# Grouped attention with normalization on one core: the inverses' transfers, the first batch's normalization, the last batch's sums and the general path rewritten

## The chip, the cores and the metric

The kernel runs on one core of a Trainium2 chip. The metric is the device time of one execution in microseconds (us). Before the change it is 1826.72 us, the median of 4 runs (1825.81 to 1828.08).

The engines are named as in the profile: PE is TensorE (its weight loads are listed apart, as PEld), DVE is VectorE, ACT is ScalarE, POOL is GpSimd, and SP is SyncE, which here issues transfers. A q behind a name (SPq) marks what the engine's sequencer does itself: it issues a transfer, waits for a semaphore, branches.

## What is computed

The input x has 32 batches of 256 channels and 32 x 32 positions. Each batch is normalized in 32 groups of 8 channels, projected to queries, keys and values of 8 heads of 32 channels, and goes through causal attention that also hides the position itself. The result is added to x. All of it is in float32.

```python
x = x + _L0_conv_ref(_gn(x), q_w, q_b, kv_w, kv_b)

def _gn(v, G=32, eps=1e-5):
    g = v.reshape(B_, G, C_ // G, H_, W_)
    m = jnp.mean(g, axis=(2, 3, 4), keepdims=True)
    s = jnp.var(g, axis=(2, 3, 4), keepdims=True)
    return ((g - m) / jnp.sqrt(s + eps)).reshape(v.shape)

def _L0_conv_ref(x, q_w, q_b, kv_w, kv_b):      # N_HEADS = 8, MASK_CENTER = True
    q = jnp.einsum('oc,bcs->bos', q_w, xf) + q_b[None, :, None]
    kv = jnp.einsum('oc,bcs->bos', kv_w, xf) + kv_b[None, :, None]
    ...
    mask = jnp.tril(jnp.ones((S, S), dtype=x.dtype), -int(MASK_CENTER))
    scores = jnp.einsum('bhqd,bhkd->bhqk', q, k) / jnp.sqrt(jnp.asarray(dk, x.dtype))
    scores = jnp.where(mask == 0, jnp.asarray(-10000.0, x.dtype), scores)
    attn = jax.nn.softmax(scores, axis=-1)
    attn = jnp.where(mask == 0, jnp.asarray(0.0, x.dtype), attn)
    out = jnp.einsum('bhqk,bhkd->bhqd', attn, v)
```

## The kernel before

**Two paths.** The function `unshifted` computes every batch with plain exponentials, without a maximum taken off first. It checks on the way that all sums of exponentials lie within 1e-20 and 1e20, and ends with the count `outside` of partitions where one doesn't. Each engine reads that count (line 784). If it is over zero, the general path `shifted` computes everything again, with the maximum taken off (line 785). With the inputs given here the count is zero, so `shifted` is jumped over. Its instructions stand in the program between that branch and the closing barrier.

**The tiling.** Channels lie on the 128 partitions, in two groups g of four heads each. The 1024 positions are two halves hf of 512 queries, and eight blocks k of 128 keys. One quarter n of a batch is a pair (g, hf), so n runs from 0 to 3. Scores are held transposed, with keys on partitions, so that their exponentials e can be multiplied with the values at once.

**Visits.** A batch is worked through in N = 12 visits, six for each group (line 531 on). A visit takes a full piece and a half piece of the scores: f is a list of pieces by half and key block, h holds half pieces. For one group the full and half pieces are (f00, f02), (f01, h10), (f10, h11), (f13, h20), (f14, h21), (f15, f16), where the first digit is the half and the second the key block, or the key block and the part for h. The multiplication with the values follows one visit later, by the list `products`. So visits 6 to 11 belong to the second group.

**The order of work.** The engines' order is written by hand: `when(i, f)` puts a step into visit i, behind that visit's scores (`at`) or behind its value products (`after`). A visit number counts from the batch's first one. PE, DVE, ACT and POOL follow that order strictly. SP takes transfers in the order of the program.

**The normalization of a batch.** DVE takes means and variances by channel (lines 167 and 168). PE averages them over each group of 8 by a product with `avg` (tile pm). ACT writes the mean with its sign changed (line 175), DVE the spread of the channels (dev, lines 183 to 187), PE averages that (tile pv), and POOL raises the variance to the power -0.5 (line 205 or 207), which gives rstd. Batch 0 has forms of its own: DVE takes the variance out of the averaging product (line 197), ACT prepares `less_mean` for one of the four pieces (line 583) and scales it (line 219), and DVE writes the other three pieces of xn (line 221). Between these PE turns the three weight matrices (`turn_weights`, four transposes each, line 136), the first of them ahead of the variance's product. `keep_busy(n)` gives PE n products without use (line 143).

**Sums of exponentials.** For batches 0 to 30 DVE adds the pieces of a quarter as they come (line 377). POOL's transfers fold the 128 partitions' sums of a quarter to 32 rows (`fold`, line 393), SP's stack the four quarters in one tile (`stack`, line 399), and DVE sums the rest (lines 406 and 407). `invert` takes the inverses (line 445) and turns them (line 447). SP writes them to DRAM in four transfers (line 450) and reads them back in sixteen, four for each quarter, each spread over 32 partitions (line 458). The four tiles rb have one buffer each. `finish` multiplies the numerators with rb on DVE (line 490), adds the bias and x (line 491) and has SP write the quarter out (line 494). The steps of batch b reach into the visits of batch b + 1: `invert` at its visit 8, the finishes behind its visits 13 to 15. For batch 30 all of this is some visits earlier.

**The last batch, 31.** There PE sums the pieces listed in `by_pe` itself, by products with a column of ones spread to 32 (`sum_keys`, line 414, tiles pd), and DVE the others. A `None` in the lists of `sums` stands for what DVE has added up. `invert_here` takes the inverses of one quarter on DVE alone, without a transfer (lines 478, 480, 481). Quarter 0 is multiplied on POOL (`quotient_aside`, line 500) and finished on ACT (`out_aside`). `end_last` inverts quarter 3 in two parts, finishes one, checks the inverses (lines 438 and 439), takes the minimum, has PE add up the result over partitions (line 523), finishes the other part, and writes `outside` (line 526).

Of the kernel before, what the change touches and what calls it, by code (L numbers as in the profile page):

```python
# [17 lines left out]
P = 128  # L18
HD = 32
# [12 lines left out]
def tile_norm_attention_residual(  # L32
# [65 lines left out]
    def unshifted():  # L98
# [71 lines left out]
        def norm_mean(b):  # L170
            mv = live["mv", b]
            pm = misc(f"pm_{b}")
            product(pm[:, :NG], avg, mv[:, :, 0])
            mean = small.tile([P, NG], F32, tag="mean", name=f"mean_{b}")
            nc.scalar.activation(mean, pm[:, :NG], AF.Identity, scale=-1.0)
            live["minus_mean", b], live["pm"] = mean, pm

        def norm_deviation(b):
# [3 lines left out]
            if b == 0:  # L182
                nc.vector.tensor_sub(dev, mv[:, :, 0], live["pm"][:, :NG])
            else:
                nc.vector.tensor_add(dev, mv[:, :, 0], minus_mean)
# [4 lines left out]
        def norm_variance(b):  # L190
            pv = misc(f"pv_{b}")
            product(pv[:, :NG], avg, live.pop(("dev", b)))
            rstd = small.tile([P, NG], F32, tag="rstd", name=f"rstd_{b}")
            live["rstd", b] = rstd
            if b == 0:

                nc.vector.tensor_scalar_add(rstd, pv[:, :NG], 1e-5)
                return
            nc.scalar.activation(rstd, pv[:, :NG], AF.Identity, bias=eps)

        def norm_rstd(b):
            rstd = live["rstd", b]
            if b == 0:

                nc.gpsimd.tensor_tensor(rstd, rstd, power, ALU.pow)
                return
# [4 lines left out]
        def norm_apply(b, hf, g):  # L211
# [6 lines left out]
            if (b, hf, g) == (0, 0, 1):  # L218
                nc.scalar.activation(xn, live["less_mean"], AF.Identity, scale=rstd)
            elif b == 0:  # L220
# [220 lines left out]
        def invert(b):  # L441
# [6 lines left out]
            spread = dram.tile([4, 4, HALF], F32, tag="inv", name=f"inverses_{b}")  # L448
            for n in range(4):
                nc.sync.dma_start(  # L450
                    out=spread[n].rearrange("(a j) (m c) -> (j m) a c", a=2, c=HD),
                    in_=turned[n * HD : (n + 1) * HD].rearrange("p (a c) -> p a c", a=2),
                )
            for n in range(4):

                rb = inverses(b, n)
                for j in range(4):
                    nc.sync.dma_start(  # L458
                        out=rb[j * HD : (j + 1) * HD], in_=spread[n, j : j + 1].broadcast_to([HD, HALF]),
                    )  # L460

        def inverses(b, n):
            if (b, n) == (B - 2, 3):
                live["rb_last"] = work.tile([P, 4, HALF], F32, tag="folded", bufs=1, name="rb_last")
            if (b, n) < (B - 2, 3) or (b, n) == (B - 1, 0):
                live["rb", b, n] = work.tile([P, HALF], F32, tag="rb", bufs=4, name=f"rb_{b}_{n}")
            else:
                live["rb", b, n] = live["rb_last"][:, n if b == B - 1 else 0, :]
            return live["rb", b, n]

        def invert_here(b, n, within=slice(0, HALF)):


            if within.start == 0:
                inverses(b, n)
# [6 lines left out]
                live["rb", b, n][:, within].rearrange("p (k r) -> p k r", r=HD),  # L482
# [3 lines left out]
        def finish(b, n, within=slice(0, HALF)):  # L486
            g, hf = divmod(n, NH)
            cols = slice(hf * HALF + within.start, hf * HALF + within.stop)
            num, rb, xt = live["num", b, n], live["rb", b, n][:, within], live["x", b]
# [6 lines left out]
        def quotient_aside(b, n):  # L496

            g, hf = divmod(n, NH)
            rb = live["rb", b, n]
# [3 lines left out]
        def out_aside(b, n):  # L503
            g, hf = divmod(n, NH)
            cols = slice(hf * HALF, (hf + 1) * HALF)
            rb = live["rb", b, n]
# [5 lines left out]
        def end_last(b):  # L512
# [4 lines left out]
            finish(b, 3, both[1])  # L517
# [6 lines left out]
            finish(b, 3, both[0])  # L524
# [19 lines left out]
        by_pe = [pc for n, m in ((5, 0), (6, 1), (7, 0), (9, 1), (10, 0), (11, 0)) for pc in products[n][m:]]  # L544
# [24 lines left out]
        with tc.manual_schedule(engines={ENG.PE, ENG.Activation, ENG.DVE, ENG.Pool}):  # L569
# [8 lines left out]
            for g in range(NG):  # L578
                norm_channels(0, g)
            norm_mean(0)  # L580

            live["less_mean"] = work.tile([P, 4, HALF], F32, tag="folded", bufs=1, name="less_mean")[:, 0, :]
            nc.scalar.activation(
                live["less_mean"], live["x", 0][:, 1, :HALF], AF.Identity, bias=live["minus_mean", 0][:, 1:2]
            )
            turn_weights(0)
            norm_deviation(0)
            norm_variance(0)
            norm_rstd(0)
            for hf in range(NH):  # L590
                for g in range(NG):
                    norm_apply(0, hf, g)
                if hf == 0:
                    for n in (1, 2):
                        turn_weights(n)
                    keep_busy(3)
# [9 lines left out]
            for b in range(B):  # L606
# [7 lines left out]
                if not last:  # L614
# [10 lines left out]
                    for n in every:  # L625
                        when(first + ((N + 9, N + 9, N + 10, N + 10) if late else FINISH)[n], lambda b=b, n=n: finish(b, n), after)
                else:
                    when(first + 3, lambda: sums(0, [None], False), after)
                    when(first + 7, lambda: sums(1, [None, *products[5]], False), after)
                    when(first + 9, lambda: sums(2, [None, *products[6][1:], *products[7]], False), after)  # L630
                    when(first + 5, lambda b=b: invert_here(b, 0), after)
# [4 lines left out]
                    when(first + 10, lambda b=b: invert_here(b, 2), after)  # L636
                    when(first + 11, lambda b=b: finish(b, 2), after)
            for i in range(B * N + 1):
# [5 lines left out]
                if i == B * N:  # L644

                    sums(3, pcs, False)
                for pc in pcs:
                    values((i - 1) // N, pc, i <= (B - 1) * N or pc not in by_pe)
                if i == B * N - 1:
                    sums(3, [*pcs, products[9][1], None])  # L650
# [11 lines left out]
    def shifted():  # L662

        with ExitStack() as inner:
            pool = inner.enter_context(tc.tile_pool(name="g_pool", bufs=1))
            rows = inner.enter_context(tc.tile_pool(name="g_rows", bufs=2))
            ps_a = inner.enter_context(tc.tile_pool(name="g_ps_a", bufs=2, space=PSUM))
            ps_b = inner.enter_context(tc.tile_pool(name="g_ps_b", bufs=2, space=PSUM))
# [143 lines left out]
```

## Time and profile before

| what | before |
|---|---|
| median of 4 runs | 1826.72 us (1825.81 to 1828.08) |
| the profiled execution | 1825.96 us, its span 1824.3 us |
| PE busy | 1810.7 us, 99% of the span |
| DVE busy | 1650.4 us, 90% |
| ACT busy | 1479.9 us, 81% |
| POOL busy | 798.4 us, 44% |
| rb read back (line 458) | 492 transfers of 64.0 KB, 2.7 us from issue to landing |
| inverses written (line 450) | 124 transfers of 8.0 KB, 2.7 us |

The span is the time from the first to the last instruction in the trace, and the execution's own time has 1.7 us more around it. A row of the timeline reads: start in us, time taken in us, engine, line of the kernel, operation, the tile written <- the tiles read, shapes, and in brackets the idle time before it with what ended it. The page's groups of instructions give count and mean duration for a line. The chain of waits follows back from the last instruction to what released each step. "Granted clock" is the share of its full clock that the throttle gives PE; here it is 0.998 over the span.

### The profile page before, as it was taken

What the parts mean: (1) busy time and instruction counts of PE and PEld (TensorE: products, weight loads), DVE (VectorE), ACT (ScalarE), POOL (GpSimd) and SP (SyncE); (2) the same over time, 40 slices, a digit from 0 to 9 for tenths busy, and PEclk for the clock granted to TensorE, in tenths of its full rate; (3) what the DMA queues carried; (4) which work ended last, traced back from release to release, by engine and by line L of the source; (5) the groups of instructions that cost most, each with busy time, mean ns of one, the idle gap of its engine ahead of it and who ended that gap; (6) DMA issues with size and microseconds to landing.
All of it is one profiled execution on the core that took longest, in us unless ns stands there. A gap on an engine that the chain in (4) does not pass through costs nothing.

```text
span 1824.3 us, 54461 instructions
## 1 busy us (share of the span) xinstructions
PE 1810.7 (99%) x23210; PEld 926.5 (51%) x23210; DVE 1650.4 (90%) x1759; ACT 1479.9 (81%) x1862; POOL 798.4 (44%) x776
## 2 busy tenths in 40 slices
PE   9999999999999999999999999999999999999997
PEld 5554555555554555545555545555454555555543
DVE  4699999999999999999999999999999999999987
ACT  6888878888778888788887888887888878888785
POOL 1453443535434445344354354443443544534432
PEclk9999999999999999999999999999999999999999
DMA  3457676676776676766767667767666676676662
GB/s 122 74 98 135 134 146 116 130 143 129 143 132 126 135 133 133 155 112 129 141 134 144 120 131 137 132 139 147 120 132 133 135 148 116 131 142 130 121 123 73
DMA packets 85226, 235.08 MB, mean 129 GB/s; under 512 B 27760, under 2 KB 28784, under 8 KB 69104
## 3 DMA queue, kind: packets, MB, share of 16 engines
q0 software_dynamic: 15872, 97.53, 39.8%
q1 hardware_dynamic: 69104, 133.99, 26.0%
q8 instruction: 184, 3.01, 0.7%
q14 instruction: 66, 0.54, 0.1%
HBM read 66.85 MB, written 34.57 MB: 56 GB/s over the span
## 4 chain that ended last, share of the span: by engine, by line
PE 97%; DVE 2%; DMA 0%; SPq 0%; issue 0%; ACT 0%; DVEq 0%
PE sT L283 31%; PE acc L369 27%; PE pp L157 26%; PE ppv L157 13%; DVE e L377 0%; SPq L458 0%; DMA rb<-inverses 0%; DMA x<-in_x_dram 0%; PE pv L157 0%; DVE rb_last L491 0%; DVE rows L407 0%; DVE turned L406 0%; DVE st L167 0%; DVE rb_last L490 0%; DVE turned L478 0%
## 5 line engine op out<-in xcount | busy, mean ns | idle before, releaser
L344 ACT ACTIVATE e<-sT 128x1024 f32<-128x1024 f32 x768 | 744.8, 1022 | 270.6 <-PE sT L283 219.5
L377 DVE TENSOR_TENSOR e<-e,e 128x1536 f32<-128x1536 f32 x377 | 633.2, 1680 | 18.4 <-POOL shift L209 0.5
L377 DVE TENSOR_TENSOR e<-e,eh 128x1024 f32<-128x1024 f32 x379 | 522.7, 1393 | 123.6 <-PE acc L369 102.2
L297 POOL TENSOR_SCALAR_AFFINE_SELECT e<-e 128x512 f32<-128x512 f32 (+1 forms) x257 | 378.3, 1472 | 556.6 <-ACT e L344 553.4
L283 PE MATMUL sT<-q,k 32*128 32x256 f32 (+3 forms) x7168 | 606.8, 458 | 0.0
L283 PEld LDWEIGHTS sT<-q,k 32*128 32x128 f32 x7168 | 444.8, 184 | 152.9 <-ACT eh L342 65.2
L157 PE MATMUL pp<-xn,wT 128*32 128x512 f32 x4096 | 492.2, 598 | 0.0
L369 PE MATMUL acc<-e,v 128*32 128x512 f32 (+2 forms) x4096 | 400.7, 486 | 0.0
L342 ACT ACTIVATE eh<-sT 128x1024 f32<-128x1024 f32 x384 | 396.3, 1032 | 0.0
L393 POOL DMA_DIRECT2D e<-e x248 | 203.0, 826 | 395.0 <-DMA e<-e 278.1
L157 PE MATMUL ppv<-wT,xn 128*32 128x256 f32 x4096 | 247.5, 382 | 0.0
L369 PEld LDWEIGHTS acc<-e,v 128*32 128x32 f32 x4096 | 132.6, 110 | 223.3 <-issue 191.5
L369 PE MATMUL acc<-eh,v 128*32 128x256 f32 x3072 | 224.4, 379 | 0.0
L157 PEld LDWEIGHTS pp<-xn,wT 128*32 128x32 f32 x4096 | 107.2, 109 | 219.4 <-issue 205.7
L369 PEld LDWEIGHTS acc<-eh,v 128*32 128x32 f32 x3072 | 98.5, 110 | 164.2 <-issue 153.2
L157 PEld LDWEIGHTS ppv<-wT,xn 128*32 128x32 f32 x4096 | 120.4, 109 | 102.7 <-issue 32.4
L297 POOL TENSOR_SCALAR_AFFINE_SELECT eh<-eh 128x512 f32<-128x512 f32 x128 | 167.3, 1307 | 0.3
L223 ACT ACTIVATE xn<-x,shift,rstd 128x512 f32<-128x512 f32 x124 | 102.9, 830 | 0.0
L491 DVE SCALAR_TENSOR_TENSOR rb<-rb,v_bias_col,x 128x512 f32<-128x512 f32 x123 | 92.7, 754 | 4.4
L237 ACT ACTIVATE k<-pp,qk_bias 128x512 f32<-128x512 f32 x128 | 89.4, 699 | 2.2 <-PE pm L157 1.1
L237 ACT ACTIVATE q<-pp,qk_bias 128x512 f32<-128x512 f32 x128 | 89.6, 700 | 1.0 <-PE pp L157 1.0
L407 DVE TENSOR_REDUCE rows<-turned 128x16 f32<-128x512 f32 x124 | 85.1, 686 | 4.3
(75 smaller groups left out, 667.0 us busy)
## 6 DMA issues: line engine op xcount, KB each, us to landing
e<-e POOLq DMA_DIRECT2D x124, 512.0 KB, 6.0
x<-in_x_dram SPq DMA_DIRECT2D x64, 512.0 KB, 6.2
e<-e POOLq DMA_DIRECT2D x124, 256.0 KB, 4.6
folded<-e SPq DMA_DIRECT2D x124, 256.0 KB, 3.0
out_dram<-rb SPq DMA_DIRECT2D x124, 256.0 KB, 4.5
rb<-inverses SPq DMA_DIRECT2D x492, 64.0 KB, 2.7
inverses<-inv_turned SPq DMA_DIRECT2D x124, 8.0 KB, 2.7
out_dram<-rb_last SPq DMA_DIRECT2D x3, 256.0 KB, 2.0
```

The costliest lines, as they stand in the source:

```text
L157: nc.tensor.matmul(out[part], lhsT=lhsT[:, part], rhs=rhs, start=start, stop=stop, skip_group_check=True)
L223: nc.scalar.activation(xn, xt, AF.Identity, bias=live["shift", b][:, g : g + 1], scale=rstd)
L237: nc.scalar.activation(live[key][:, cols], pp, AF.Identity, bias=qk_bias[:, n, g : g + 1], scale=(SCALE, 1.0)[n],)
L283: return nc.tensor.matmul(pair[:, cols], lhsT=live["k", b, g][rows, kb * P : (kb + 1) * P], rhs=live["q", b, g][rows, hf * HALF + of.start ...
L297: nc.gpsimd.affine_select(out=diagonal, in_=diagonal, pattern=[[0, heads.stop - heads.start], [0, n], [1, P]], compare_op=ALU.is_gt, fill= ...
L342: exp = nc.scalar.activation(eh.rearrange("p (n bank) q -> p bank n q", n=2), short, AF.Exp)
L344: nc.scalar.activation(e[:, 2 * a : 2 * a + 2, :], pairs[a], AF.Exp)
L369: nc.tensor.matmul(acc[HD * j : HD * (j + 1), of], lhsT=live["v", b][:, kb, h * HD : (h + 1) * HD], rhs=e[:, j, cols], start=first, stop=l ...
L377: nc.vector.tensor_add(total[:, :, of], total[:, :, of], e[:, :, cols])
L393: nc.gpsimd.dma_start(out=total[:rows], in_=total[rows : 2 * rows], accum_op=ALU.add)
L407: nc.vector.tensor_reduce(live["rows", b][:, j * HALF // HD : (j + 1) * HALF // HD], turned.rearrange("p (k r) -> p k r", r=HD), AX.X, ALU ...
L491: nc.vector.scalar_tensor_tensor(rb, rb, v_bias_col[:, g : g + 1], xt[:, g, cols], ALU.add, ALU.add)
```

## The change

- **Start.** The special forms of batch 0 go, except that DVE still writes xn, now all four pieces. The variance comes to ACT, the product `shift` is formed on POOL as in other batches, and all three `turn_weights` stand behind `norm_rstd`, with a `keep_busy(3)` ahead of the variance and one behind the weights.
- **Inverses.** One transfer writes them to DRAM and four read them back, one for each of the four head rows, into one tile rb of all quarters with one buffer. The last batch uses a tile of the tag `folded` for all its quarters.
- **Last batch.** f13 of the second group is summed by PE in place of DVE, and f02 by DVE in place of PE. The sums for quarter 3 are made in another order. Quarter 0 is inverted one visit later, quarter 2 ahead of the value products of its visit in place of behind them. In `end_last` both finishes come ahead of the check.
- **General path.** It is written in loops over value blocks, groups, q and k, query blocks, heads and key blocks, with 14 matrix products in the text, in place of one loop over batches around code that is written out.

```diff
@@ norm_deviation, norm_variance, norm_rstd, norm_apply
-            if b == 0:
-                nc.vector.tensor_sub(dev, mv[:, :, 0], live["pm"][:, :NG])
-            else:
-                nc.vector.tensor_add(dev, mv[:, :, 0], minus_mean)
+            nc.vector.tensor_add(dev, mv[:, :, 0], minus_mean)
...
+            nc.scalar.activation(rstd, pv[:, :NG], AF.Identity, bias=eps)
             live["rstd", b] = rstd
-            if b == 0:
-
-                nc.vector.tensor_scalar_add(rstd, pv[:, :NG], 1e-5)
-                return
-            nc.scalar.activation(rstd, pv[:, :NG], AF.Identity, bias=eps)
...
-            if (b, hf, g) == (0, 0, 1):
-                nc.scalar.activation(xn, live["less_mean"], AF.Identity, scale=rstd)
-            elif b == 0:
+            if b == 0:
                 nc.vector.tensor_scalar(xn, xt, live["minus_mean", b][:, g : g + 1], rstd, ALU.add, ALU.mult)
@@ invert
-            spread = dram.tile([4, 4, HALF], F32, tag="inv", name=f"inverses_{b}")
-            for n in range(4):
+            spread = dram.tile([2, 4, 2, HALF], F32, tag="inv", name=f"inverses_{b}")
+            nc.sync.dma_start(
+                out=spread.rearrange("a n j (m c) -> (n j m) a c", c=HD), in_=turned.rearrange("p (a c) -> p a c", a=2),
+            )
+            live["rb", b] = work.tile([P, 4, HALF], F32, tag="rb", bufs=1, name=f"rb_{b}")
+            for h in range(4):
                 nc.sync.dma_start(
-                    out=spread[n].rearrange("(a j) (m c) -> (j m) a c", a=2, c=HD),
-                    in_=turned[n * HD : (n + 1) * HD].rearrange("p (a c) -> p a c", a=2),
+                    out=live["rb", b][h * HD : (h + 1) * HD],
+                    in_=spread[h // 2, :, h % 2, :].unsqueeze(0).broadcast_to([HD, 4, HALF]),
                 )
-            for n in range(4):
-
-                rb = inverses(b, n)
-                for j in range(4):
-                    nc.sync.dma_start(
-                        out=rb[j * HD : (j + 1) * HD], in_=spread[n, j : j + 1].broadcast_to([HD, HALF]),
-                    )
...
@@ end_last
-            finish(b, 3, both[1])
+            for part in both:
+                finish(b, 3, part)
...
             nc.tensor.matmul(pc[0:1, 0:1], lhsT=worst, rhs=ones, start=True, stop=True)
-            finish(b, 3, both[0])
@@ the visits
-        by_pe = [pc for n, m in ((5, 0), (6, 1), (7, 0), (9, 1), (10, 0), (11, 0)) for pc in products[n][m:]]
+        by_pe = [pc for n, m in ((5, 0), (7, 0), (9, 0), (10, 0), (11, 0)) for pc in products[n][m:]]
@@ the start
             norm_mean(0)
-
-            live["less_mean"] = work.tile([P, 4, HALF], F32, tag="folded", bufs=1, name="less_mean")[:, 0, :]
-            nc.scalar.activation(
-                live["less_mean"], live["x", 0][:, 1, :HALF], AF.Identity, bias=live["minus_mean", 0][:, 1:2]
-            )
-            turn_weights(0)
+            keep_busy(3)
             norm_deviation(0)
             norm_variance(0)
             norm_rstd(0)
+            for n in range(3):
+                turn_weights(n)
+            keep_busy(3)
             for hf in range(NH):
                 for g in range(NG):
                     norm_apply(0, hf, g)
                 if hf == 0:
-                    for n in (1, 2):
-                        turn_weights(n)
-                    keep_busy(3)
@@ the last batch's steps
-                    when(first + 9, lambda: sums(2, [None, *products[6][1:], *products[7]], False), after)
-                    when(first + 5, lambda b=b: invert_here(b, 0), after)
+                    when(first + 9, lambda: sums(2, [None, *products[7]], False), after)
+                    when(first + 6, lambda b=b: invert_here(b, 0), after)
...
-                    when(first + 10, lambda b=b: invert_here(b, 2), after)
+                    when(first + 10, lambda b=b: invert_here(b, 2))
...
+                if i == B * N - 1:
+                    sums(3, [None, *products[9]])
                 for pc in pcs:
                     values((i - 1) // N, pc, i <= (B - 1) * N or pc not in by_pe)
                 if i == B * N - 1:
-                    sums(3, [*pcs, products[9][1], None])
+                    sums(3, pcs)
@@ shifted: the loops (their bodies left out)
             with tc.For_i(0, B, 1) as b:
...
-                for k in range(NB):
+                with tc.For_i(0, NB, 1) as k:
...
-                for g in range(NG):
-                    qk = []
-                    for n in range(2):
+                with tc.For_i(0, NG, 1) as g:
+                    qk = pool.tile([P, 2 * S], F32, name="g_qk")
+                    with tc.For_i(0, 2, 1) as n:
...
-                    for i in range(NB):
-                        n_k = (i + 1) * P
-                        acc = ps_c.tile([P, HALF], F32, tag="c", name="g_acc")
-                        for j in range(4):
+                    with tc.For_i(0, NB, 1) as i, tc.For_i(0, 4, 1) as j:
...
+                        with tc.For_i(0, NB, 1) as k:
```

## The prediction

> **What bounds the kernel now.** I read the page first, then the stretches, the chain of waits at both ends, and the rows of the line that holds the closing branch. From the page:
>
> ```profile
> span 1824.3 us, 54461 instructions
> PE 1810.7 (99%) x23210; PEld 926.5 (51%) x23210; DVE 1650.4 (90%) x1759; ACT 1479.9 (81%) x1862; POOL 798.4 (44%) x776
> ...
> q8 instruction: 184, 3.01, 0.7%
> q14 instruction: 66, 0.54, 0.1%
> ...
> PE 97%; DVE 2%; DMA 0%; SPq 0%; issue 0%; ACT 0%; DVEq 0%
> ```
>
> TensorE carries 97% of the chain. The stretches say where it doesn't: one batch in the middle, and the last 24 us (columns: stretch, its length, busy time of each engine with its count, granted clock, DMA share, GB/s).
>
> ```profile
> 900.00:956.00 56.00, 56.00 (x724) 28.60 (x724) 52.00 (x56) 46.15 (x59) 25.05 (x24) 1.00 0.69 134
> ...
> 1800.00:1824.00 24.00, 13.77 (x182) 6.97 (x174) 17.73 (x32) 6.65 (x8) 5.33 (x4) 0.84 0.34 114
> ```
>
> In the middle TensorE is busy 56.00 of 56.00 us at clock 1.00 and DVE has 4.0 us spare; nothing that only moves DMAs or DVE work shows there unless it makes TensorE wait. So the two ends decide. The start, in order of time:
>
> ```profile
> 8.85 0.16 DVE L197 TENSOR_SCALAR rstd<-pv 128x2 f32<-128x2 f32 x1 [0.45 <-PE pv L157]
> 9.10 0.71 POOL L205 TENSOR_TENSOR rstd<-rstd,power 128x2 f32<-128x2 f32 x1 [6.65 <-DVE rstd L197]
> ...
> 9.66 0.83 PE L143 MATMUL busy<-ident 128*128 128x128 f32 x6
> ...
> 10.54 3.64 PE L157 MATMUL pp<-xn,wT 128*32 128x512 f32 x32
> ```
>
> TensorE starts the projections at 10.54, when its own filler ends, not when xn (DVE, 9.84 + 0.55) is there. The end:
>
> ```profile
> 1793.31 1.75 SPq L450 DMA_DIRECT2D inverses<-inv_turned  x4
> ...
> 1803.92 2.29 DVE L377 TENSOR_TENSOR e<-e,e 128x2048 f32<-128x2048 f32 x1
> ...
> 1811.67 0.61 PE L414 MATMUL pd<-eh,pick 128*32 128x256 f32 x8
> ...
> 1813.74 0.44 DVE L478 STREAM_TRANSPOSE turned<-pd 128x256 f32<-128x256 f32 x1
> ...
> 1818.41 0.14 DVE L526 TENSOR_SCALAR outside<-pc 1x1 int32<-1x1 f32 x1
> ```
>
> The last denominators (pd) are whole at 1812.3, but DVE comes to them at 1813.74, without a gap since 1798.57: DVE bounds the end. After it, the rows of the branch over the general path (engine, operation; first and last start):
>
> ```profile
> L785 PEldq COMPARE_BRANCH  x1: 3969/3969/3969, 1819.2 to 1819.2; - x1
> ...
> L785 SPq COMPARE_BRANCH  x1: 45/45/45, 1819.8 to 1819.8; - x1
> L785 ACTq EVENT_SEMAPHORE  x1: 17/17/17, 1822.9 to 1822.9; - x1
> L785 DVEq EVENT_SEMAPHORE  x1: 21/21/21, 1823.0 to 1823.0; - x1
> ```
>
> ACT and DVE branch at 1819.1 and 1819.2 and go on 3.7 us later; SP branches at 1819.8 and goes on at 1820.3. The span's last 5.8 us are this jump and the closing barrier.
>
> **The start.** TensorE loses the four transposes it did while waiting for dev, gets them back after the variance, and has a new filler of 3 before it. From the end of pv (8.80 in the chain): 12 transposes at 1.03/8 = 0.129 us are 1.55, the filler 0.67 (the chain's own piece), so the projections start near 11.06 in place of 10.54: **+0.52**. The other way in is shorter: rstd on ACT takes 0.28 (its row at L199) in place of 0.16 on DVE, so POOL ends near 9.9 and xn's first half is there at 10.5; its second, now also on DVE, at 11.0, first needed 0.86 after the start. The new shift product on POOL (0.20) and the dropped less_mean (0.72 on ACT) have nobody behind them. The low bound is the xn path (+0.1), the high one all of this in a row (+1.0); I take 0.52, as TensorE's own queue ends last.
>
> **The middle.** Of 20 SP issues a batch 5 remain, with the same bytes. Finish of quarter 0 now waits for all four returns. The issue rows are 0.34 to 1.80 us for one; landing medians 2.7 (8 KB write, 64 KB read), 3.0 (folded, 256 KB), 4.5 (out, 256 KB), 6.2 (x, 512 KB). No row has a 32 KB write or a 256 KB read of the inverses: low, 2.7 + three issues of 0.46 + 3.0 = 7.1 us from write to last return; high, 4.5 + 1.4 + 6.2 = 12.1; I take the low one, since folded's 256 KB on the same queue is the nearest in size and queue, and either end gives the same here. In the batch shown the write goes at 901.39 and DVE first uses a result at 924.52: 23.1 us, so at least 11 are spare. The one rb buffer is free once its last output lands (issued 936.0, + 4.5), and is next written after 957.4. On SP, folded and the outputs behind the returns only move forward. **0**; without that cover each us of lateness would cost DVE one, 4.0 a batch being its spare.
>
> **The last batches.** The sum of f13 on DVE (2.29) becomes a TensorE sum; f02's add (1.22, its usual row) comes to DVE at visit 7 and falls into the 2.15 us in which DVE waits at 1796.4; TensorE loses f02's sum. Four heads of 512 cost TensorE 0.86 (pd groups start at 1808.23 and 1809.09), of 256 0.43. So at visit 9 TensorE is 0.43 earlier, and at the end 0.86 longer: pd whole at 1812.7 instead of 1812.3. DVE: from 1800.93, finishes 0 and 1 (3.1), inversion of quarter 2 now before the others (1.7), finishes 2 and 3 (3.0 alone, 4.3 beside POOL's masks as now), finish of the last batch's quarter 2 (1.65): free at 1810.4 to 1811.7. TensorE now decides, and the last inversions start at 1812.7, **1.0 earlier**. Inverting quarter 0 one visit later (1.7 of DVE, traded with equal work) pushes POOL's two products (2.57) to 1791.1 and the mask behind them to about 1794.9, when TensorE wants it: 0 to 0.6 lost there; I take 0.
>
> In the closing steps both finishes now precede the check: inversions 2.3, finishes 1.9, check and minimum 0.7, the TensorE hop 0.4, outside 0.2 = 5.5 against 4.8 now, when the second finish covers the hop. So outside comes 1.0 - 0.7 = **0.3 earlier**; the last output is issued 1.5 earlier, which nothing waits for as long as the jump takes 3.7.
>
> **The jump.** The page's two instruction queues give the measure: 46420 TensorE instructions in 3.01 MB are 65 bytes each, so a q14 packet (8.2 KB) holds about 128. In the assembled program of the kernel before, the skipped path is 170 instructions on ACT, 855 on DVE, 39 on POOL and 51 on SP, 43 of SP's being the frame of one loop. In the trace ACT stands 102 instructions behind its last packet when it jumps (target 272: late), SP 96 (target 147: not late). The new path has seven loops: SP's is at least 7 x 43 = 301, further than the jump that was late. So SP is late too: it reads outside 0.6 earlier (0.3 as above, 0.3 because no output issue stands before it), branches 0.43 later, waits 3.7, and has still its 1.05 us of semaphore steps, which ACT's wait hid: it drains near 1824.0 instead of 1823.4: **+0.6**. Bounds: no engine late, -2.6 (output landing and SP's steps then end last); SP late and a further packet needed at once, +2.8.
>
> [...]
>
> **Sum.** +0.52 + 0 + 0.6 = +1.1 on the profiled execution's 1825.96 (span 1824.3 and 1.7 around it): 1827.1. The median of the runs, 1826.72, lies 0.76 above; with the same distance 1827.8.
>
> **Rivals.** *The jump becomes free*: the loops keep every target in reach. For it: SP and POOL, with short paths, lose nothing now. Against it: ACT was late at 272 and the loops give it over 170. -2.6 + 0.5: 1824.6.
> *Returns late at the end (slower)*: the four 256 KB returns of the next-to-last batch hold DVE at its first finish. The write goes at 1793.3; the low bound brings them at 1800.4, before DVE is free, the high one at 1805.4. DVE's spare before TensorE decides is 1.0 to 2.3, so it counts from about 1802.5, one for one: 2.9 at the high bound, 1830.7. For it: the 64 KB returns took 3.9 there. Against it: that stretch has a DMA share of 0.13.
> *A second packet after the jump (slower)*: SP's target lies within its last 25 or so instructions of a packet, and the next is only fetched 0.6 after it resumes; +2.2 more, 1830.0.
>
> **Numbers.** Forecast 0.70, free jump 0.10, late returns 0.10, second packet 0.10. A difference under 0.2% (3.65 us) is about what a measurement here can't tell from none. The free jump stays within it unless the start is also cheaper (faster 0.05); most of the late returns and half of the second packet go over it, and I add 0.08 for a TensorE stall in the middle, which 31 batches would multiply (slower 0.20); same 0.75. Range 1824.5 to 1831.0, from the free jump to the late returns; the forecast's own is 1826.5 to 1829.5.
>
> **What would show it.** Right: projections start near 11.1; 56.0 of 56.0 in the middle; no 2.29 add at the end, transposes of the last pd near 1813.2 (start included); SP's event at the branch 3.7 us behind its branch. Wrong: idle TensorE in the middle, DVE waiting for rb, or ACT and SP going on at once.

## The result, and the profile after

| what | before | after |
|---|---|---|
| median of the runs | 1826.49 us (60 runs, 1825.81 to 1828.21) | 1828.97 us (40 runs, 1827.49 to 1831.03) |
| the profiled execution | 1825.96 us, span 1824.3 us | 1827.85 us, span 1826.0 us |

The ratio after/before is 1.0011, with an interval from 1.0007 to 1.0016: 0.1% slower, less than the 0.2% that the prediction set as the bound of what can be told from no change. The forecast was 1827.8 us.

From the page of after: the span, the engines, the two instruction queues, the chain's shares, and the two DMA groups of the inverses (count, KB each, median us from issue to landing).

```profile
span 1826.0 us, 53754 instructions
PE 1812.0 (99%) x23216; PEld 926.8 (51%) x23216; DVE 1647.5 (90%) x1759; ACT 1478.9 (81%) x1861; POOL 796.0 (44%) x777
...
q8 instruction: 183, 3.00, 0.7%
q14 instruction: 62, 0.51, 0.1%
...
PE 98%; DVE 1%; POOL 0%; DMA 0%; issue 0%; ACT 0%; DVEq 0%
...
rb<-inverses SPq DMA_DIRECT2D x124, 256.0 KB, 7.9
...
inverses<-inv_turned SPq DMA_DIRECT2D x31, 32.0 KB, 1.9
```

TensorE still carries the chain. POOL has come into it, with less than a percent of the span; the next views show where. The stretches of after (columns as before):

```profile
900.00:956.00 56.00, 56.00 (x728) 28.59 (x720) 51.91 (x56) 46.15 (x59) 25.05 (x24) 1.00 0.71 134
...
1800.00:1826.00 26.00, 15.80 (x206) 7.63 (x195) 16.50 (x32) 8.10 (x9) 3.00 (x4) 0.87 0.29 93
```

The middle is what it was: TensorE busy 56.00 of 56.00 us. The start of after, in order of time:

```profile
7.54 0.24 PE L157 MATMUL pm<-mv,avg 128*32 128x2 f32 x8 [0.82 <-DVE mv L168]
...
8.91 1.53 PE L136 MATMUL wt<-ident,wn 128*128 128x128 f32 x12
...
10.20 1.00 DVE L208 TENSOR_SCALAR xn<-x,mean,rstd 128x512 f32<-128x512 f32 x2 [1.60 <-POOL rstd L196]
...
10.28 0.90 PE L143 MATMUL busy<-ident 128*128 128x128 f32 x6
11.11 0.16 PEld L157 LDWEIGHTS pp<-xn,wT 128*32 128x32 f32 x8
11.11 0.64 PE L157 MATMUL pp<-xn,wT 128*32 128x512 f32 x4
```

The projections start when TensorE's own queue of transposes and filler ends, while xn's first piece (10.20, two pieces in 1.00) is there by then. The end of after, in order of time:

```profile
1791.77 1.27 POOL L476 TENSOR_TENSOR rb_last<-num,rb_last 128x512 f32<-128x512 f32 x1 [3.48 <-DVE rb_last L457]
...
1793.12 1.27 POOL L477 TENSOR_TENSOR rb_last<-rb_last,x 128x512 f32<-128x512 f32 x1
...
1793.80 1.68 DVE L364 TENSOR_TENSOR e<-e,eh 128x1024 f32<-128x1024 f32 x1
...
1794.35 2.09 POOL L284 TENSOR_SCALAR_AFFINE_SELECT e<-e 128x1024 f32<-128x1024 f32 x1
...
1796.49 1.07 PE L356 MATMUL acc<-e,v 128*32 128x384 f32 x16 [0.81 <-POOL e L284]
...
1802.71 0.69 DVE L466 TENSOR_TENSOR rb<-num,rb 128x512 f32<-128x512 f32 x1 [0.17 <-DMA out_dram<-rb_last]
...
1814.39 0.45 DVE L454 STREAM_TRANSPOSE turned<-pd 128x256 f32<-128x256 f32 x1 [1.61 <-PE pd L401]
...
1819.31 0.15 DVE L502 TENSOR_SCALAR outside<-pc 1x1 int32<-1x1 f32 x1 [0.37 <-PE pc L500]
```

At 1814.39 DVE has waited 1.61 us for the last denominators: TensorE decides the end now, where DVE did before. But TensorE itself waited 0.81 us at 1796.49 for a causal mask on POOL. That mask stands behind quarter 0's two products, and took 2.09 us; before, it took 1.10:

```profile
1791.10 1.10 POOL L297 TENSOR_SCALAR_AFFINE_SELECT e<-e 128x1024 f32<-128x1024 f32 x1
```

The rows of the branch in after, which is line 778 there:

```profile
L778 SPq EVENT_SEMAPHORE  x3: 17/17/17, 1824.1 to 1824.3; - x3
L778 ACTq COMPARE_BRANCH  x1: 50/50/50, 1820.0 to 1820.0; - x1
...
L778 PEldq COMPARE_BRANCH  x1: 479/479/479, 1820.1 to 1820.1; - x1
L778 DVEq COMPARE_BRANCH  x1: 72/72/72, 1820.1 to 1820.1; - x1
L778 SPq COMPARE_BRANCH  x1: 45/45/45, 1820.3 to 1820.3; - x1
...
L778 PEldq EVENT_SEMAPHORE  x1: 51/51/51, 1820.6 to 1820.6; - x1
L778 DVEq EVENT_SEMAPHORE  x1: 21/21/21, 1820.7 to 1820.7; - x1
L778 ACTq EVENT_SEMAPHORE  x1: 17/17/17, 1824.0 to 1824.0; - x1
```

ACT is late as before. DVE and TensorE, late before, go on after 0.6 us. SP, in time before, is late now: it branches at 1820.35 and its three semaphore steps (the first row) start at 1824.1, 3.75 us later.

Put end to end, the two profiled executions differ by 1.71 us:

| stretch | before, us | after, us | difference |
|---|---|---|---|
| start of the span to pm (the first load's landing) | 7.35 | 7.54 | +0.18 |
| pm to the first projection | 3.18 | 3.57 | +0.39 |
| first projection to the last inversions | 1803.20 | 1803.28 | +0.08 |
| last inversions to the end of `outside` | 4.81 | 5.07 | +0.26 |
| end of `outside` to the end of the span | 5.71 | 6.51 | +0.80 |

The first row is no part of the change: pm starts between 7.22 and 7.75 over all executions profiled here, without regard to the edit. The experiments take the other four apart.

### The profile page after: what moved, and what is told of

The parts are those of the page before. It is cut to its first block, busy times and chain, and to the rows that moved or that the text cites. A ratio compares the mean times of both kernels' runs of the same rounds, so it can differ in the third digit from the quotient of the medians.

```text
span 1826.0 us, 53754 instructions
## 1 busy us (share of the span) xinstructions
PE 1812.0 (99%) x23216; PEld 926.8 (51%) x23216; DVE 1647.5 (90%) x1759; ACT 1478.9 (81%) x1861; POOL 796.0 (44%) x777
## 4 chain that ended last, share of the span: by engine, by line
PE 98%; DVE 1%; POOL 0%; DMA 0%; issue 0%; ACT 0%; DVEq 0%
PE sT L270 31%; PE acc L356 27%; PE pp L157 26%; PE ppv L157 13%; PE pd L401 0%; DVE e L364 0%; DMA x<-in_x_dram 0%; PE pv L157 0%; DVE rows L394 0%; DVE turned L393 0%; DVE st L167 0%; POOL e L284 0%; PE pm L157 0%; DVE rb_last L457 0%; PE busy L143 0%
```

## The experiments

Each is an edit of after, unless it says before. Stretches are those of the table; a ratio is to before on the same chip. Each kernel computes the whole reference.

**e1: the start undone.**

```diff
-            keep_busy(3)
...
+            turn_weights(0)
             norm_deviation(0)
...
-            for n in range(3):
-                turn_weights(n)
-            keep_busy(3)
```

> Changed kernel with batch 0's normalization and weight turns as before. Theory (the start costs 0.4 to 0.6 us, all of it TensorE's own queue of 12 transposes and a filler): projections start near 10.6 instead of 11.1 us, the last inversions near 1813.9 instead of 1814.4, span 1825.5. Rival (the start is hidden further on, since ACT ends the wait near 28 us in both): the projections start earlier but the last inversions stay near 1814.4 and the span at 1826.0.

Measured: median 1828.79 us (11 runs), ratio 1.0011 (1.0002 to 1.0020); span 1826.8. From pm to the projections it took 4.10 us, where before takes 3.18 with the same steps; from there to the last inversions 1803.29, as in after. The row of the twelve weight transposes in e1 (min/median/max ns):

```profile
L136 PE MATMUL wt<-ident,wn x12: 417/418/476, 7.9 to 10.7; 128*128 128x128 f32 x12
```

In before and in after that row has a median of 273; before's:

```profile
L136 PE MATMUL wt<-ident,wn x12: 272/273/331, 7.5 to 9.5; 128*128 128x128 f32 x12
```

So the same transposes took 1.53 times as long, in a stretch where the view's granted clock reads 1.00 (the last section says what that reading is worth). No theory had this; it hides the few tenths that e1 was to show, and e7, e8 and e10 follow it up.

**e2: quarter 0's product on POOL one visit later.**

```diff
-                    when(first + 6, lambda b=b: quotient_aside(b, 0), after)
+                    when(first + 7, lambda b=b: quotient_aside(b, 0), after)
```

> Changed kernel with the quotient of the last batch's quarter 0 put behind visit 7 instead of visit 6 on GpSimd, so that the mask of visit 7 goes first. Theory (TensorE waited 1.0 us for that mask behind the two products): no wait of TensorE for the mask at 1796, the last inversions near 1813.4, span 1825.0. Rival 1 (the mask itself is slow, 2.09 instead of 1.10, because it shares with DVE's add of f02): half of the wait stays, span 1825.5. Rival 2 (DVE, held by the late returns, decides next): the last inversions stay near 1814.4.

Measured: span 1825.0 us, median 1826.93 (11 runs), ratio 1.0003 (0.9994 to 1.0012). First projection to last inversions: 1802.26, 1.02 less than after and 0.94 less than before. Its timeline, POOL:

```profile
1790.46 1.10 POOL L284 TENSOR_SCALAR_AFFINE_SELECT e<-e 128x1024 f32<-128x1024 f32 x1 [2.31 <-ACT e L331]
1791.63 1.27 POOL L476 TENSOR_TENSOR rb_last<-num,rb_last 128x512 f32<-128x512 f32 x1
1792.98 1.27 POOL L477 TENSOR_TENSOR rb_last<-rb_last,x 128x512 f32<-128x512 f32 x1
```

and TensorE:

```profile
1793.61 1.92 PE L157 MATMUL pp<-xn,wT 128*32 128x512 f32 x16
1795.35 1.05 PE L356 MATMUL acc<-e,v 128*32 128x384 f32 x16
```

With the mask ahead of the products it takes 1.10 us, and the value product follows the projection without a gap: 1.74 us from start to start, 2.74 in after. So the mask's lateness is the whole 1.0 us, and the new order of the last batches is worth 0.94 us where nothing takes it back. The late returns of the second rival show as well, but cost nothing here: DVE's first finish waits 1.23 us.

```profile
1802.61 0.69 DVE L466 TENSOR_TENSOR rb<-num,rb 128x512 f32<-128x512 f32 x1 [1.23 <-DMA out_dram<-rb_last]
```

The transfer that the row names landed at 1802.74 by the trace, after this start; the last of the four returns, for which DVE waited as well, landed at 1802.32. DVE still waits 0.55 us for TensorE at the last inversions.

**e3: targets of the jump brought nearer.** Sixty instructions without effect on ACT and forty on SP, ahead of the first load's use, shift where the branch stands in its packet of instructions (some 128, the prediction's estimate from the bytes of the two instruction queues). In the built program ACT's target falls from 279 instructions behind the start of its packet to 211, SP's from 307 to 219.

```diff
             nc.scalar.activation(junk, ones, AF.Exp)
+            for _ in range(60):
+                nc.scalar.drain()
+            for _ in range(40):
+                nc.sync.drain()
```

> Changed kernel with 60 drains more on ACT and 40 more on SP near the start, which move both engines' place in their 128-instruction packets at the closing branch, so that each target lies within 256 instructions of the start of the packet it branches from (ACT 211 instead of 279, SP 219 instead of 307). No other work differs. Theory (the jump is late by packet position alone): ACT and SP go on within 0.5 us of their branches, SP drains near 1821.9 instead of 1825.1, span 1822.8. Rival (what counts is the distance jumped, 208 and 205 instructions, or the loops): both still go on 3.7 us later, span 1826.0.

Measured: span 1822.9 us, median 1826.23 (11 runs), ratio 0.9998 (0.9989 to 1.0007). End of `outside` to the end: 3.26, 3.25 less than after. Rows of its branch (line 782 there):

```profile
L782 SPq EVENT_SEMAPHORE  x3: 17/17/17, 1821.1 to 1821.2; - x3
L782 ACTq COMPARE_BRANCH  x1: 50/50/50, 1820.2 to 1820.2; - x1
...
L782 SPq COMPARE_BRANCH  x1: 50/50/50, 1820.6 to 1820.6; - x1
L782 ACTq EVENT_SEMAPHORE  x1: 17/17/17, 1820.7 to 1820.7; - x1
```

Both are through in half a microsecond. The 3.25 us are the price of late targets alone, since nothing between branch and barrier was changed.

**e4: the general path written out, as in before.**

```diff
-                with tc.For_i(0, NB, 1) as k:
+                for k in range(NB):
...
```

> Changed kernel with the general path of before (written out, not executed). Theory: SP (51 instructions) and, by its new place, ACT (170, target at 241) are in reach, TensorE and DVE are late, as SP's own steps no longer come after its wait: SP drains 4.85 us behind outside, as before the change, span 1825.2. Rival (the late returns or the closing order make the end longer, not the path): span 1826.0.

Measured: span 1824.6 us, median 1827.07 (11 runs), ratio 1.0005 (0.9996 to 1.0014). End of `outside` to the end: 5.41, 1.1 less than after. SP goes on after 0.49 us. Of its branch (line 759 there):

```profile
L759 PEldq COMPARE_BRANCH  x1: 3671/3671/3671, 1819.8 to 1819.8; - x1
L759 DVEq COMPARE_BRANCH  x1: 72/72/72, 1819.9 to 1819.9; - x1
...
L759 ACTq EVENT_SEMAPHORE  x1: 17/17/17, 1822.8 to 1822.8; - x1
L759 DVEq EVENT_SEMAPHORE  x1: 21/21/21, 1823.3 to 1823.3; - x1
```

So the loops are what made SP late and TensorE prompt: it goes on after 0.54 to 0.55 us in every profile with loops, and after 3.7 to 4.0 us in those without. DVE is not settled by this: with the same loops it goes on after 0.56 us in after and after 3.98 us in e5. A miss: ACT was expected in time at 241 instructions, and came 3.07 us late.

**e5: the inverses' transfers as in before** (four writes, sixteen reads), into after's tile.

```diff
...
-            for h in range(4):
...
-                    in_=spread[h // 2, :, h % 2, :].unsqueeze(0).broadcast_to([HD, 4, HALF]),
...
+            for n in range(4):
+                for j in range(4):
+                    nc.sync.dma_start(
+                        out=live["rb", b][j * HD : (j + 1) * HD, n, :], in_=spread[n, j : j + 1].broadcast_to([HD, HALF]),
+                    )
```

> Changed kernel with the inverses written in 4 and read back in 16 transfers again, into the one tile of the change. Theory (the transfers cost nothing in the middle, and at the end DVE has spare): TensorE busy 56.0 of 56.0 us in the middle, from the start of the projections to the last inversions 1803.3 us as in the changed kernel, span 1826.0 (SP and ACT late after the jump as before). Rival (the 256 KB returns, which take 7.9 us to land, hold DVE and so TensorE): that stretch shorter by 0.5 us or more.

Measured: median 1828.34 us (11 runs, lowest 1827.84), ratio 1.0010 (1.0001 to 1.0019); span 1827.9. First projection to last inversions: 1803.28, the same as after to 0.01 us. The start took 5.12 us from pm to the projections, with transposes of 421 ns, which is most of why the span is longer. Between the projections and the last inversions the transfers cost and bring nothing.

**e6: before, with the loops alone.**

```diff
-                for k in range(NB):
+                with tc.For_i(0, NB, 1) as k:
...
```

> The kernel before with the general path in loops and nothing else changed. Theory (the jump's price goes by which engine is out of reach, and SP is, at 91 + 205): SP goes on 3.7 to 4.0 us behind its branch, the time from outside to the end of the span 6.5 instead of 5.7 us, span 1825.1 or 0.8 us more than before. Rival (loops make the jump shorter for DVE and TensorE and so the end shorter): 5.0 us or less.

Measured: median 1828.79 us (11 runs), ratio 1.0009 (1.0000 to 1.0018); span 1827.1. End of `outside` to the end: 6.82, 1.11 more than before, with SP 3.68 us behind its branch, ACT 4.00, DVE 4.14. The loops alone bring the whole of the change's loss there. SP branches 0.37 us later behind `outside` than in after, as an output's issue stands in front of it; but the end also varies by itself, from 6.51 to 6.75 us in the five profiles with after's closing steps and with ACT and SP late (after, e1, e2, e5, e8), so little can be made of the other 0.3. The rest of the span is the start (4.35 us, transposes of up to 417 ns), with 0.34 us more in the first projections behind it, and a first load that was 0.17 later.

**e7 and e8: before and after, each with two more filler products ahead of pm** (13 in place of 11).

```diff
-            keep_busy(11)
+            keep_busy(13)
```

> The kernel before with two more filler products ahead of the first averaging product (13 instead of 11), which shorten TensorE's idle time at 6.7 to 7.4 us. Theory (the times of the kernel before lie in two groups near 1826.0 and 1827.5 since TensorE's clock drops to half for some 3 us in some executions when that idle time falls badly, as in the profile of e1_start_undone, where a transpose took 418 ns in place of 273): one group near 1826.0, median 0.5 us below that of before. Rival (the groups come from the first load or from the host): two groups as before, the median the same.

> Changed kernel with the same longer filler, 13 products in place of 11. Theory: one group near 1827.9, 1.9 us above e7_before_longer_filler, which is the span's difference between the two profiled executions (1.7 us) within 0.3; so the rest of the 2.5 us between the medians of the two kernels is a different share of slow-clock executions. Rival: the difference to e7 stays 2.5 us.

Measured: before with it 1826.12 us (11 runs, ten of them from 1825.86 to 1826.23; ratio 0.9996, 0.9987 to 1.0005), after with it 1827.90 (11 runs, 1827.49 to 1828.30; ratio 1.0004, 0.9995 to 1.0014). Spans 1824.4 and 1826.0, as without it. The reason given for it did not hold: TensorE's idle time ahead of pm is 1.05 us in e7's profile and 0.63 in before's. The plain kernels' times fall in two groups each: before's 1825.5 to 1826.6 and 1826.9 to 1828.7 over the runs beside these experiments; after's, less sharply, 1827.5 to 1828.2 and 1828.4 to 1829.9, with two runs above. With the longer filler, but for one run, only the lower groups are left. Their difference, 1.78 us, is what the change costs with that choice taken out, and agrees with the 1.71 of the spans.

**e10: before with a shorter filler** (`keep_busy(8)`), the other way round.

> The kernel before with 8 fillers ahead of the first averaging product in place of 11, so TensorE idles some 2 us there instead of 0.6. Theory (the slow group is TensorE's clock dropping in that idle time): all or nearly all runs in the slow group, near 1827.5, transposes at 418 ns. Rival (the groups have another cause): two groups as before.

Measured: median 1827.74 us, and none of 10 runs below 1827.01, where 10 of 21 runs of before beside it lie from 1825.71 to 1826.24; ratio 1.0006 (0.9997 to 1.0015). The transposes' row in it:

```profile
L136 PE MATMUL wt<-ident,wn x12: 421/421/476, 7.4 to 10.3; 128*128 128x128 f32 x12
```

Less filler, slow transposes, and the upper group alone. e7 and e10 together show that the upper group is TensorE's pace at the start, which the amount of filler moves.

**e11: ACT's target at 241 again**, by 90 instructions on ACT and not by the written-out path (which e4 had). It is e3 with this edit:

```diff
-            for _ in range(60):
+            for _ in range(90):
                 nc.scalar.drain()
```

> As e3_targets_in_reach, but with 90 drains on ACT in place of 60, which put ACT's target at 241 where it was late in e4_path_written_out, while DVE's at 238 and GpSimd's at 251 were in time. Theory (reach is counted alike for all engines and 256 is its end, and e4 was late for another cause): ACT goes on within 0.5 us, span 1822.9. Rival (ACT's reach ends lower, or its place is known only to some 15 instructions): ACT goes on 3 to 4 us later, span 1825.2.

Measured, one execution: 1826.68 us, span 1824.2. ACT goes on 0.45 us behind its branch; end of `outside` to the end 3.26, as in e3. So 241 is not beyond reach in itself, and why ACT was late in e4 stays open; three engines were late at once there, and no run here separates that from the path. In this execution, with after's filler of 11, the start took 4.89 us, with transposes of 272 to 476 ns.

**e12: the order of the closing steps undone.**

```diff
-            for part in both:
-                finish(b, 3, part)
+            finish(b, 3, both[1])
...
+            finish(b, 3, both[0])
             outside = const.tile([1, 1], I32, name="outside")
```

> Changed kernel with the last two finishes on either side of the check again. Theory: from the last inversions to outside 4.8 us instead of 5.1, but SP, which issues the last output just before it reads outside, branches later by about the same, so the span stays within 0.2 of the changed kernel's (at equal start). Rival (the order is worth the 0.7 us of the forecast): span 0.6 less.

Measured, one execution: 1828.24 us, span 1826.3. Last inversions to the end of `outside` 4.83 (after 5.07), from there to the end 6.85 (after 6.51): 11.68 in all against 11.58. The new order brings `outside` 0.24 later and SP's branch 0.37 earlier behind it (0.89 after `outside` instead of 1.26), and so is worth 0.1 us here as long as SP is the last. That is less than the end varies by itself (6.51 to 6.75 us), so it can't be told from nothing.

**e9: the parts that pay, joined.** After with e1's start, e2's later product, e3's instructions and e7's filler.

```diff
-            keep_busy(11)
+            keep_busy(13)
...
-                    when(first + 6, lambda b=b: quotient_aside(b, 0), after)
+                    when(first + 7, lambda b=b: quotient_aside(b, 0), after)
...
+            for _ in range(60):
+                nc.scalar.drain()
+            for _ in range(40):
+                nc.sync.drain()
```

> The changed kernel with what the runs so far point to, all together: batch 0's start as before with a filler of 13, the quotient of quarter 0 behind visit 7, and the drains that bring SP's and ACT's targets in reach. Theory (the terms add up: -0.4, -1.0 and -3.25 on the changed kernel's span of 1826.0): span 1821.3, all runs in one group near 1823.2, 2.7 us under the fast group of before. Rival (the terms hide one another, as DVE, 1.6 us ahead of TensorE at the end, becomes the bound once the mask's wait is gone): span over 1822.3.

Measured: median 1823.56 us (11 runs, 1823.13 to 1824.01), before 1827.14 (21 runs); ratio 0.9982 (0.9973 to 0.9991). Span 1821.4. It beats both kernels. Its last inversions on DVE:

```profile
1813.05 0.45 DVE L467 STREAM_TRANSPOSE turned<-pd 128x256 f32<-128x256 f32 x1 [0.61 <-PE pd L414]
```

From the projections (10.79) that is 1802.26 as in e2; pm to the projections takes 3.18 as in before, and the end 3.26 as in e3. The three savings add up.

## Why the prediction held, point by point

- **The start, +0.52: right in kind, measured +0.39.** TensorE's own queue ended last, and the projections came at 11.11 (forecast near 11.06; the terms as written, 8.80 + 1.55 + 0.67, make 11.02), but 0.18 of that is a later pm. At the full pace, pm to projections is 3.18 us in the three profiles with before's order (before, e7, e9) and 3.57 to 3.63 in the six with after's (after, e2, e3, e4, e8, e12). e1 alone wouldn't have shown it.
- **The middle, 0: right.** e5 shows it to 0.01 us. The size behind it was wrong: one return of 256 KB took 7.9 us to land, above even the 6.2 taken for it in the high bound. In the batch shown, the four returns were issued from 904.08 to 906.73 and landed 5.0 to 10.4 us later, the last at 916.5 by the trace; DVE first uses one at 925.11, so 8.6 us of cover were left of the 11 that were named.
- **The last batches, 1.0 earlier: the gain is there, and the term that was put at nothing takes it back.** The text had "0 to 0.6 lost there; I take 0" for the mask behind POOL's products. Measured: 1.02 lost (e2). Its start was right: 1793.7 by the text's sum, 1794.3 with the start's 0.57 added, and 1794.35 in the trace. Its length was not: 2.09 us in place of 1.10, beside DVE's add of f02. At 1.10 it would have ended at 1795.45, ahead of 1795.68, when TensorE began to wait for it. The text had moved that add into just this stretch, and priced the mask by its row elsewhere. That TensorE and no longer DVE decides the last inversions was right (DVE waits 1.61).
- The mask's lengthening goes with DVE's add beside it, though no run takes away this one add alone: of the 127 masks of 128 x 1024 in after's trace, the 30 with no add of exponentials beside them took 1.10 us each, and every longer one, up to 2.61, ran beside such an add. The add of f02 took 1.68 in place of 1.22, but not for the mask: it takes 1.68 in e2 too, at 1793.66, when the mask has long ended and POOL's second product (1792.98, 1.27 us) runs.
- **The closing steps, 5.5 for 4.8: measured 5.07 for 4.81.** The steps are in the order that was worked out, and e12, with the old order, has 4.83, so the difference is some 0.25 and not 0.7. The 5.5 was a sum of whole durations, and in after's rows most of these instructions start before the one ahead of them has ended.
- **The jump, +0.6: right in kind.** The +0.6 holds the 0.3 by which `outside` was to come earlier, so for the time from `outside` to the end the forecast was +0.9; measured +0.80, and 0.7 to 1.0 over all profiles (5.71 to 5.80 in before, e7 and e10, 6.51 to 6.75 in the five named at e6). SP is late, as e3, e4 and e6 show each in its own way. The step behind it was partly wrong: a path of at least 7 x 43 = 301 instructions on SP was counted, and the built program has 205, some 29 for each of the seven loops. SP's place, 102 in its packet, put the target at 307 all the same. The text didn't look at DVE and TensorE, which the shorter paths (205 and 204) brought into reach here; with ACT and SP late that gave nothing. For DVE it also depends on its place, as e5 and e6 have it late.
- Of the targets counted here, those at 147 instructions (SP, before), 211 and 219 (ACT and SP, e3) and 241 (ACT, e11) were in time, and those at 272 (ACT, before), 279 and 307 (ACT and SP, after) and 296 (SP, e6) late; the one at 241 in e4 was late and stays unexplained. Where the reach ends was not measured more closely, so no run shows the 256 in the texts of e3 and e11. Nor does one show what a late engine waits for; the shortest such wait named here is 3.07 us (ACT, e4), the longest 4.14 (DVE, e6).
- **The rivals.** The free jump did not come by itself, and e3 shows its worth: 3.25 us, where 2.6 and the 0.6 of the forecast were named, 3.2 together. Late returns: they came near to counting. The last of the four was issued at 1796.81 and landed at 1802.42, 5.6 us later, just ahead of DVE's first finish at 1802.71. The row there names an output's transfer for a wait of 0.17 us, but that landed at 1802.82, after the start; so DVE did wait for rb, a sign that the text gives for being wrong, and it cost nothing, as TensorE decided later. The 3.9 us that spoke for this rival was the longest landing of before's sixteen returns there, not a usual one: their median was 2.1. A second packet: none; no engine waited again after it went on.
- **The sum: near by luck.** By stretch the text had +0.52, -1.0, +0.7 and +0.9, in all +1.1. Measured in the spans: 0.39 + 0.08 + 0.26 + 0.80 = 1.53 (1.71 with the later pm), and 1.78 between the medians of e7 and e8. The last batches missed by 1.08 us one way, and the closing steps (0.44), the start (0.13) and the jump (0.10) the other way, so errors of the terms hid one another. The median moved by 2.5 us and not 1.8, because more of after's executions have the slow start (27 of its 40 runs lie in the upper group, 29 of before's 60) and it costs after more.

## What to carry to other kernels

When an edit moves work between engines at a stretch that decides, price the moved instruction by what will run beside it, not by its row elsewhere; a mask that took 1.10 us alone took 2.09 beside an add. Code that is never run still has a price, where engines jump over it at the end: 3.25 us here, and a hundred instructions without effect, put where the engines wait anyway, took it away. When a kernel's times fall in two groups, compare each edit's spans by stretch, and look for what is decided before the kernel's main part; a median over both groups moves with their shares.

## What the hardware showed that was not expected

TensorE's pace at the start differs between executions of one kernel: transposes of 128 x 128 took 273 ns in some and 417 to 421 in others. The granted clock does show it, if one knows where to look. The trace's record of the clock begins only where full speed is first granted, and ahead of that the views read 1.00. It begins between 4.74 and 7.83 us where the transposes are fast, and at 10.68, 11.08 and 11.29 us in e10, e1 and e11. The products change their pace just there. In e4 the record begins at 5.30, and the filler's products take 421 ns each before it and 275 behind it; in e1 the last transposes before 11.08 still take 417. In e5 and e6 full speed comes early, at 5.68 and 5.74, holds for 3.41 us, and is then taken back to half for 3.41 us, from 9.09 and 9.15. A view of e5 with narrow stretches (columns as before) has this:

```profile
9.00:10.00 1.00, 1.00 (x12) 0.98 (x13) 0.00 (x0) 0.26 (x1) 0.34 (x1) 0.55 1.03 369
10.00:11.00 1.00, 1.00 (x7) 1.00 (x6) 0.59 (x2) 0.58 (x1) 0.57 (x2) 0.50 1.01 414
```

With before's order this makes pm to the projections 4.10 to 4.35 us long in place of 3.18 (e1, e10, e6), with after's 4.89 to 5.12 in place of 3.57 (e11, e5): after has more TensorE work in that stretch, and so loses more. How long TensorE had been idle before pm does not decide it: 1.33 us in e9 with transposes of 273, 0.93 in e1 with 418. So the theory of e7 and e10, a clock that drops in that idle time, does not describe e1, e10 and e11, where full speed had not been granted yet. The half clock for some 3 us that e7's text names is in the records of e5 and e6, for 3.41 us, but behind pm (7.75 and 7.53) and not ahead of it.

No run shows what makes the first grant come early or late, or what takes the clock back. Measured is that it differs between executions of one kernel, and with the amount of filler: none of 10 runs with a filler of 8 is in the lower group (e10), and ten of 11 with a filler of 13 are (e7). In the 3.41 us before the clock was taken back, TensorE was busy for 1.85 us in e5 and 1.82 in e6. In e9, e4 and e7 it was busy for 2.08, 2.12 and 2.35 us in the 3.41 us behind the first grant, and kept the clock. By these five profiles, how busy TensorE is in that stretch may decide whether it keeps the clock, but no run varied that alone.

Open remain what made ACT late in e4 and DVE in e5 and e6, and how much filler would exclude the slow start for good: one of the eleven runs of e7 is still in the upper group.
